# Adding the attention row on GpSimd, evicting it on VectorE, and new due times for the first tiles

## The chip, the cores and the metric

The kernel runs on one core of one Trainium2 chip. The metric is the device time of one execution in microseconds (us), median of several runs; lower is better. The engines are named PE (TensorE), DVE or V (VectorE), ACT (ScalarE), POOL or G (GpSimd) and SP (SyncE, which here issues DMAs). PSUM is the memory that PE writes its products to, SBUF the working memory of all engines.

## What is computed

64 sequences of 128 tokens with 256 features pass one layer of two steps:

```python
# attention step: q, k, v are 16 features wide; correlation over time, 12 best shifts, softmax weights w
q = LN(x) @ Wq + bq;  k = v = ctx @ Wq + bq
corr = mean over batch and feature of ifft(fft(q) * conj(fft(k)))
R = sum over the 12 best shifts of w * roll(v, -shift)      # the same for all 16 heads
x = x + (R repeated 16 times) @ Wout + bout
# feed-forward step; fp4(.) rounds blocks of 16 numbers to a 4-bit grid with one scale per block
xq = fp4(LN(x));  h = silu(xq @ fp4(w_gate).T) * (xq @ fp4(w_up).T)     # 704 wide
x = x + fp4(h) @ fp4(w_down).T
```

Because of the reshape in `R` (batch, heads, 16, time) to (batch, time, 256), the attention step adds to each token a row that depends on few indices only: in this kernel's layout it is one of four matrices `O[0]` to `O[3]`, each 128 x 256 with one more column that holds its mean.

## The kernel before

**Three stages.** In the first (0 to about 55 us) the inputs `xt` and `cx` are read, q, k and the correlation are built on PE, and the weights of the feed-forward step are quantised and transposed. In the second (about 55 to 72 us) the correlation is turned into shifts and weights (`E`, `wm`, `inv`), the weights meet the output matrix (`Wp`), the values are copied from PSUM by ACT (`Va`, L1504), and PE forms the four matrices `O[g]` (L1581). `O[0]` is evicted from PSUM by V, as product times `inv` plus the bias row `Bo` (L1594). For `O[1]` to `O[3]` the bias is brought in by one more product on PE, with one row as its inner size (L1572), and ACT evicts with the scale `inv` (L1588). Before its `Va` copies of g = 1 to 3, ACT loads its table for square roots (L1553); later it loads the table for Silu (L1625).

**The third stage** handles 64 tiles of 128 rows (tile t is row block t % 4 of `X[t // 4]`, and uses `O[(t // 4) % 4]`).

- x part of a group of tiles (`x_parts`): `neg` is minus the new mean (L461); `cc` is x + O + neg. For tiles 0 and 1 (`fast`) V makes `cc` from x and O in one instruction (L472), and x + O itself is added apart. For all others O is first added to `X` (by V at L447 for tiles 2 to 11, two tiles an instruction; by an accumulating DMA issued on GpSimd's queue at L483 from tile 12 on), and ACT makes `cc` (L499). ACT squares and sums (L509), V takes block maxima (`am` L519), reciprocals (`rz` L558), scales `cc` (L586), ACT or V rounds (`k`), V multiplies by the block scales (`xhl` L615). The result is transposed, by PE for tiles 0 to 3 (L631, copied from PSUM at L637 by V for tiles 0 and 1 and by ACT for 2 and 3), by DMA on SP's queue for the rest (L644).
- per tile (`group_ops`): 18 products `gu` on PE (L1224) into one of two PSUM buffers; ACT's Silu gives `g` (L1230); V forms `h` (L1237), which frees the PSUM buffer; V's block maxima `hs` (L1247) read 88 pad columns of `h` that hold a least value, written once per buffer of `h` by three ACT instructions (L1605, key "least"); V's reciprocal `hr` (L1261); GpSimd scales `h` (L1276; V does so for tile 0 and the last ones); ACT rounds (`hk`, `hc`), V multiplies by the scales (`hl` L1329), SP's DMA transposes it into one of eight buffers `hT`, 17 products `pd` on PE (L1373, L1375) follow, V adds to `X` (L1392), SP stores.

**What sets the order.** Nothing runs in the order in which it is written. `S.op(engine, cost, ...)` records each operation with a cost in ns, its reads and writes and a due time `dl`; due times are carried back along the dependences; `plan` then walks through a planned clock and gives each engine, of what is ready within 400 ns, the operation that is due first (operations due inside a window of `RUSH` can hold a place free). `after` is an order without a wait, `chain` forces an operation to follow another on the same engine, `rel` is an earliest time, `late` adds to the planned ready time. Each engine then runs its list in order, and semaphores do the waiting. Where PE's plan has a gap, filler products with `ident` (L726) are written into it.

The due times of the third stage come from one line, with `T0` = 58000, `SLOT` = 5425 and `t` the tile: `at(t) = T0 + SLOT * t`, 4000 earlier for tiles 0 and 1. `gu` of tile t is due at `at(t)`; `pd` is due 4.5 slots later, growing by 6 slots up to tile 56. The x parts are due at 58000 (tiles 0, 1), 65200 (2, 3), 73000 (4 to 7, in one piece), and then by `at`.

Of the kernel before, what the change touches and what calls it, by code (L numbers as in the profile page):

```python
# [23 lines left out]
P = 128  # L24
# [20 lines left out]
WAIT = 400.0  # L45
RUSH = ((10000.0, 40000.0), (41000.0, 73000.0))
SPARE = 400.0
# [213 lines left out]
def xattn_ffn(ctx: ExitStack, tc: tile.TileContext, x, xt, cx, wo, bo, wgu, wd, out):  # L261
# [78 lines left out]
    SLOT = 5425.0  # L340
    LC = 4.5
    GROW = 6.0
# [17 lines left out]
    LA = 4000.0  # L360
    BEFORE = 16
    HOT2 = 70000.0
    ZV, CV, EV = (0, *range(62, 64)), range(61, 64), range(64)
    HPE = (63,)
    GROUPS = [(0,), (1,), *((t, t + 1) for t in range(2, 62, 2)), (62,), (63,)]
    DUE1 = 15000.0
    Q1 = ((0, 4, 0.0, False),)
    TD = 54000.0
# [56 lines left out]

    def x_parts(R, q, i0, nt, fast, due, alu, pe_x=False, root=False, both=None, off=0):
        g, hq = q % 4, q // 4
# [12 lines left out]

        eng = "V"
        pe = fast

        def add(lo, hi):
            def f():
                v = Xq.t[:, i0 + lo : i0 + hi]
                (V if eng == "V" else G).tensor_tensor(v, v, O[g][:, 0:D].unsqueeze(1).broadcast_to([P, hi - lo, D]), ALU.add)  # L447
# [19 lines left out]
        for i in tiles:  # L467
            if fast:
                op(
                    "V",  # L470
                    336,
                    lambda i=i: V.scalar_tensor_tensor(  # L472
                        T["cc"].t[:, i], Xq.t[:, i0 + i], T["neg"].t[:, i : i + 1], O[g][:, 0:D], ALU.add, ALU.add
                    ),
                    r=[(Xq, i0 + i), T["neg"], ("O", g)],
                    w=[(T["cc"], i)],
                )
        if alu == "D":
            for i in tiles:
                adds[4 * q + i] = op(  # L480
                    "G",
                    900,
                    lambda i=i: G.dma_start(Xq.t[:, i0 + i], O[g][:, 0:D], accum_op=ALU.add),  # L483
                    r=[("O", g)],
                    w=[(Xq, i0 + i)],
                    lat=LA,
                    port=False,
                )
                adds[4 * q + i].rel = 0.0
        else:  # L490
            step = 1 if nt == 1 else 2
            for lo in range(0, nt, step):
                add(lo, lo + step)
        for i in tiles:
            if not fast:
                op(
# [664 lines left out]

    T0 = TG

# [34 lines left out]
    def group_ops(tiles):  # L1198
# [10 lines left out]
        def twice(k):  # L1209
            return sub(k).unsqueeze(3).broadcast_to([P, nt, NB, 2])  # L1210

        def at(t):
            return T0 + SLOT * t - (EARLY * (t - END) if t > END else 0.0) - (4000.0 if t < 2 else 0.0)

        for i, t in enumerate(tiles):
# [123 lines left out]
        for i, t in enumerate(tiles):  # L1339
# [30 lines left out]
            def f_d(i=i, hT=hT):  # L1370
# [27 lines left out]
        )  # L1398
        op("SP", 370, lambda: SP.dma_start(out[:, q, i0 : i0 + nt], v()), r=xk, dl=at(tiles[-1]) + SLOT * (LC + GROW * min(t, END) / 64.0 + 2), lat=LL)

# [151 lines left out]
    t1_op = op("A", 450, lambda: A.activation(Wp[:, 1], spec["J", 1][1](), AF.Copy, scale=wv[:, 1:2]), r=[(pv3, "j"), ("wv", 1)], w=[("Wp", 1)])  # L1552
    op("A", 1300, lambda: A.activation(warm, c_half, AF.Sqrt), w=["tbl"], dl=TO, after=[*quick, t1_op])  # L1553
    for e in range(2):
# [8 lines left out]
    d_parts(loaded, (w_op,))  # L1563
    load_x(1, dl=TD + 9000, after=loaded)
    for g in range(4):
        po, pn = ((pdc, "o"), lambda: pdc.t[:, 0 : D + 1]) if g == 0 else ((pa, "o", g), lambda g=g: pa.t[:, 512 * (3 - g) :][:, 0 : D + 1])
        Vg = Va[:, g].rearrange("p (b r e) -> p e (b r)", b=16, e=2)
        if g:
            op(
                "PE",  # L1570
                690,
                lambda pn=pn: PE.matmul(pn(), es[0:1, 0:1].broadcast_to([1, P]), Bo[0:1], start=True, stop=False),  # L1572
                r=["Bo", "es"],
                w=[po],
                after=quick_o,
            )
        first = [
            op(
                "PE",
                560,  # L1580
                lambda e=e, pn=pn, Vg=Vg, g=g: PE.matmul(pn(), Vg[:, e], Wp[:, e], start=(g == e == 0), stop=(e == 1)),  # L1581
                r=[("Va", g), ("Wp", e)],
                w=[po],
            )
            for e in range(2)
        ]
        if g:
            op("A", 450, lambda g=g, pn=pn: A.activation(O[g], pn(), AF.Copy, scale=inv), r=[po, "inv"], w=[("O", g)], dl=TG if g < 2 else TG + SLOT)  # L1588
        else:
            quick_o = first  # L1590
            op(
                "V",
                450,
                lambda pn=pn: V.scalar_tensor_tensor(O[0], pn(), inv, Bo, ALU.mult, ALU.add),  # L1594
                r=[po, "inv", "Bo"],
                w=[("O", 0)],
                dl=TG,
            )

    heat(lambda: hot.t[:, 384:512], (hot, "h"), TG + 7000.0, hot, after=first)  # L1600
    for t in h_tiles:
        op(
            "A",
            350,
            lambda t=t: A.activation(  # L1605
                t[:, :, NF : NF + 2 * NB], ones[:, 0 : 2 * NB].unsqueeze(1).broadcast_to([P, 2, 2 * NB]), AF.Copy, scale=htiny
            ),
            r=[("O", 3)],
            w=["least"],
        )  # L1610
    S.rel = 0.0
    for i, n, e in FIRST:
        x_stage(R4, 0, i, n, True, TG + i * STEP0, e, True, True)
    x_stage(R4, 0, 2, 2, False, TG + 2 * STEP0, "V", True, True)

# [97 lines left out]
```

## Time and profile before

| what | value |
|---|---|
| median of 3 runs | 438.35 us (436.62 to 438.74) |
| the profiled execution: its own time | 436.5 us |
| its span of instructions | 434.6 us |
| busy: PE, DVE, ACT, POOL | 96%, 90%, 66%, 32% |
| first and last product of the feed-forward step | 72.02 us, 431.12 us |
| last `gu` ends | 407.74 us |

The span is what lies between the first and the last instruction; the profiled execution's own time is 1.9 us more. PE's share of busy time includes fillers and products that run at half clock, so it is no measure of useful work: that is 64 times (18 `gu` + 17 `pd`).

### The profile page before, as it was taken

How to read it: one execution, taken by the hardware profiler on the slowest of the kernel's cores; microseconds unless marked ns; L12 is line 12 of the kernel's file. 1: busy time of each engine (PE TensorE's matmuls, PEld its weight loads, DVE VectorE, ACT ScalarE, POOL GpSimd, SP SyncE). 2: the span in 40 equal slices, each digit the busy share in tenths (PEclk: the TensorE clock that was granted, in tenths of full speed). 3: DMA queues.
4: the chain of work that ended last, by engine and by line, in shares of the span. 5: the costliest groups of instructions: out<-in, count | busy, mean ns of one | idle time of the engine just before them, and what ended most of it. 6: DMA issues, size and time to landing. Idle time of an engine off the chain costs nothing.

```text
span 434.6 us, 7990 instructions
## 1 busy us (share of the span) xinstructions
PE 418.9 (96%) x2946; PEld 268.9 (62%) x2946; DVE 392.9 (90%) x855; ACT 285.6 (66%) x480; POOL 137.3 (32%) x122
## 2 busy tenths in 40 slices
PE   8999989899889999999999999999999999999996
PEld 8557666446555656666566666666665666566685
DVE  7999597999999999899999989999999999978862
ACT  3897557978595787467856794887579576364410
POOL 1000002154344354444444444454444222314100
PEclk9999996999999999999999999999999999999999
DMA  8999999453887688489758987697669716942462
GB/s 309 416 419 419 306 224 321 61 111 79 169 151 147 162 179 190 112 134 241 148 121 165 210 141 172 144 160 157 128 151 173 147 40 133 189 116 66 103 162 74
DMA packets 152247, 76.62 MB, mean 176 GB/s; under 512 B 134160, under 2 KB 141712, under 8 KB 152208
## 3 DMA queue, kind: packets, MB, share of 16 engines
q1 hardware_dynamic: 144720, 69.29, 62.5%
q0 software_dynamic: 7488, 6.82, 11.0%
q8 instruction: 23, 0.38, 0.4%
q14 instruction: 16, 0.13, 0.1%
HBM read 27.76 MB, written 8.39 MB: 83 GB/s over the span
## 4 chain that ended last, share of the span: by engine, by line
PE 66%; DVE 16%; ACT 8%; DMA 6%; issue 2%; SPq 1%; ACTq 0%
PE gu L1224 37%; PE pd L1373 14%; PE pd L1375 8%; DMA xt<-in_xt_dram 4%; DVE hs L1247 3%; DVE h L1237 2%; DMA ct<-in_cx_dram 2%; DVE hl L1329 2%; ACT junk L509 1%; ACT g L1230 1%; ACT cc L499 1%; DVE am L519 1%; DVE cc L586 1%; PE gu L1581 1%; ACT hk L1304 1%
## 5 line engine op out<-in xcount | busy, mean ns | idle before, releaser
L1224 PE MATMUL gu<-WgH,xT 128*128 128x512 f16 (+1 forms) x768 | 191.7, 361 | 5.1 <-ACT g L1230 1.9
L1224 PEld LDWEIGHTS <-xT 128*128 128x128 f16 x1152 | 112.4, 98 | 114.5 <-issue 5.1
L1276 POOL TENSOR_TENSOR h<-h,hr 128x704 f32<-128x704 f32 x61 | 92.6, 1519 | 196.3 <-DVE hr L1261 169.3
L1224 PE MATMUL gu<-WgL,xT 128*128 128x512 f16 (+1 forms) x384 | 107.4, 361 | 0.0
L1230 ACT ACTIVATE g<-gu,ug 128x704 f32<-128x704 f32 x64 | 53.7, 840 | 42.0 <-PE gu L1224 41.9
L1304 ACT ACTIVATE hk<-h,c_half 128x1408 int16<-128x1408 f32 (+1 forms) x34 | 47.4, 1395 | 37.3 <-POOL h L1276 34.4
L1247 DVE TENSOR_REDUCE hs<-h 128x44 f32<-128x792 f32 x64 | 66.6, 1041 | 2.1
L1237 DVE SCALAR_TENSOR_TENSOR h<-gu,uh,g 128x704 f32<-128x704 f32 x64 | 55.9, 874 | 5.1 <-ACT g L1230 3.2
L483 POOL DMA_DIRECT2D X<-O x36 | 31.7, 970 | 71.7 <-ACT junk L509 71.7
L1320 ACT ACTIVATE hc<-hk,c_sub 128x1408 f16<-128x1408 int16 (+1 forms) x32 | 45.6, 1426 | 0.5
L1373 PE MATMUL pd<-WdH,hT 128*128 128x256 f16 x352 | 43.7, 273 | 1.2 <-DMA hT<-hl 1.2
L1373 PEld LDWEIGHTS <-hT 128*128 128x128 f16 x352 | 34.3, 98 | 9.5 <-DMA hT<-hl 1.6
L1329 DVE TENSOR_TENSOR hl<-hc,hsb 128x1408 f16<-128x1408 f16 (+1 forms) x34 | 28.6, 842 | 0.2
L1329 DVE TENSOR_TENSOR hl<-hc,hsl 128x1408 f16<-128x1408 f16 (+1 forms) x34 | 28.6, 841 | 0.0
L1261 DVE RECIPROCAL hr<-hs 128x44 f32<-128x44 f32 x64 | 26.8, 418 | 0.2
L509 ACT ACTIVATE junk<-cc 128x256 bf16<-128x256 f32 x64 | 26.0, 406 | 0.4 <-DVE cc L472 0.2
L1375 PE MATMUL pd<-WdL,hT 128*128 128x256 f16 x192 | 26.2, 273 | 0.0
L1290 ACT ACTIVATE hsb<-hs 128x176 bf16<-128x176 f32 (+1 forms) x34 | 11.4, 334 | 19.8 <-DVE hs L1247 19.8
L499 ACT ACTIVATE cc<-X,neg 128x256 f32<-128x256 f32 x46 | 22.5, 499 | 2.9 <-DVE neg L461 2.9
L932 ACT ACTIVATE xsq<-xt,shift 128x1024 f32<-128x1024 f32 x16 | 17.7, 1142 | 8.9 <-DVE shift L928 6.3
L586 DVE TENSOR_TENSOR cc<-cc,rz 128x256 f32<-128x256 f32 x64 | 23.3, 418 | 0.1
L1373 PE MATMUL pd<-WdH,Wdn 128*128 128x256 f16 x176 | 21.8, 273 | 0.7 <-DMA Wdn<-hl 0.7
(254 smaller groups left out, 569.4 us busy)
## 6 DMA issues: line engine op xcount, KB each, us to landing
xt<-in_xt_dram SPq DMA_DIRECT2D x16, 512.0 KB, 8.2
ct<-in_cx_dram SPq DMA_DIRECT2D x7, 1024.0 KB, 12.8
X<-in_x_dram SPq DMA_DIRECT2D x12, 512.0 KB, 4.4
out_dram<-X SPq DMA_DIRECT2D x23, 256.0 KB, 2.3
X<-O POOLq DMA_DIRECT2D x36, 128.0 KB, 3.4
XA<-in_x_dram SPq DMA_DIRECT2D x4, 512.0 KB, 5.3
XA<-O POOLq DMA_DIRECT2D x16, 128.0 KB, 2.7
out_dram<-XA SPq DMA_DIRECT2D x7, 256.0 KB, 2.0
```

Source lines behind the costliest of these rows:

```text
L483: lambda i=i: G.dma_start(Xq.t[:, i0 + i], O[g][:, 0:D], accum_op=ALU.add),
L509: lambda i=i: A.activation(T["junk"].t, T["cc"].t[:, i], AF.Square, accum_out=T["ssq"].t[:, off + i : off + i + 1]),
L1224: PE.matmul(pg.t[:, c0:c1], src[:, b], w[:, k, c0:c1], start=(m == 0), stop=(m == 5))
L1230: lambda pg=pg, g=g: A.activation(g.t, pg.t[:, 0:NF], AF.Silu, scale=ug),
L1237: lambda pg=pg, g=g, i=i: V.scalar_tensor_tensor(B["h"].t[:, i, 0:NF], pg.t[:, NF:NG], uh, g.t, ALU.mult, ALU.mult),
L1247: lambda i=i: V.tensor_reduce(B["s"].t[:, i], B["h"].t[:, i].rearrange("p (jj b e) -> p b jj e", b=NB, e=2), AX.XY, ALU.max, apply_absolut ...
L1276: lambda i=i, zv=zv: (V if zv else G).tensor_tensor(per_block(B["h"].t[:, i, 0:NF], NB), per_block(B["h"].t[:, i, 0:NF], NB), spread(B["r" ...
L1304: lambda: A.activation(sub("k"), sub("h")[:, :, 0:NF], AF.Identity, bias=c_half, scale=24.0),
L1320: lambda: A.activation(flat("c"), flat("k"), AF.Identity, bias=c_sub, scale=SUB),
L1329: lambda e=e, part=part: V.tensor_tensor(B["hl"].t[:, 0:nt, e].rearrange("p t (jj n) -> p t jj n", jj=JJ), sub("c").rearrange("p t (jj n) ...
L1373: PE.matmul(pd, hT.t[:, b], WdH[:, :, b], start=(b == 0), stop=False)
L1375: PE.matmul(pd, hT.t[:, b], WdL[:, :, b], start=False, stop=(b == 5))
```

## The change

1. **O.** The one-row bias products are gone. All four `O[g]` are formed by two products each, in the order g = 0 to 3, and evicted by V as product times `inv` plus `Bo`, due at 58000, 61000, 70000, 70000.
2. **ACT's tables.** The load for square roots no longer follows the `Va` copy of g = 0 and is due 12 us earlier; the load for Silu is due 8 us later.
3. **Adds of O.** For tiles 0 to 11 GpSimd adds O to `X`, one tile an instruction, in the order 2 to 7, 0, 1, 8 to 11 (`GORD`), then come the DMA adds of tiles 12 to 16. The three writes of the least value move from ACT to GpSimd, between the adds of tiles 7 and 0.
4. **Tiles 4 to 7** run as two x parts of two tiles, instead of one of four.
5. **Due times.** `at(t)` starts at 71000 with 3700 a tile up to tile 6, then 5425: 17 us later for tile 0, 2.65 us later from tile 6 on. `pd` is due at `down_at(t)`, 8.6 us later than before for tiles up to 56. `late` of `pd` is zero for tiles 0 to 7, and the forced chain of reciprocal, `h` and `hs` starts at tile 6. The second window of `RUSH` reaches to 90000.

The switches `C1`, `C2E`, `F2` and `cce` of the diff are off in this kernel, and `A0`, `A1`, `A2`, `Q2A` = "P" make `eng` "G" for the adds.

```diff
-RUSH = ((10000.0, 40000.0), (41000.0, 73000.0))
+RUSH = ((10000.0, 40000.0), (41000.0, 90000.0))
...
-    LC = 4.5
+    T0 = 71000.0
+    PACE = 3700.0
+    RAMP = 6
+    FILL = 20000.0
+    LX = 1000.0
+    SL0 = 8
...
+    OD = 3000.0
+    DQ = 2
+    GORD = (2,3,4,5,6,7,0,1,8,9,10,11)
+    LEAST = 5
+    CHAIN = 6
...
+    SILU = 8000.0
+    GA = 800.0
...
-    Q1 = ((0, 4, 0.0, False),)
+    Q1 = ((0,2,0.0,False),(2,2,0.0,False))
...
-        eng = "V"
+        eng = "G" if alu == "P" else "V"
...
-            op(
+            adds[4 * q + i0 + lo] = op(
                 eng,
-                (60 + 270 * n) if eng == "V" else 650 * n if n == 1 else 613 * n,
+                (60 + 270 * n) if eng == "V" else GA * n,
...
-            step = 1 if nt == 1 else 2
+            step = 1 if nt == 1 or eng == "G" else 2
...
+    def at(t):
+        return T0 + PACE * min(t, RAMP) + SLOT * max(t - RAMP, 0) - (EARLY * (t - END) if t > END else 0.0)
+
+    def down_at(t):
+        return T0 + FILL + SLOT * t + SLOT * GROW * min(t, END) / 64.0 - (EARLY * (t - END) if t > END else 0.0)
...
-            if t - 1 in recips:
+            if t - 1 in recips and t >= CHAIN:
...
-                late=SLACK if t < END else 0.0,
-                dl=at(t) + SLOT * (LC + GROW * min(t, END) / 64.0 + nt - 1 - i + (LATE if t >= END else 0)),
+                late=SLACK if SL0 <= t < END else 0.0,
+                dl=down_at(t) + SLOT * (nt - 1 - i + (LATE if t >= END else 0)),
...
-    op("A", 1300, lambda: A.activation(warm, c_half, AF.Sqrt), w=["tbl"], dl=TO, after=[*quick, t1_op])
+    op("A", 1300, lambda: A.activation(warm, c_half, AF.Sqrt), w=["tbl"], dl=TO - 12000.0, after=[t1_op])
...
-        if g:
-            op(
-                "PE",
-                690,
-                lambda pn=pn: PE.matmul(pn(), es[0:1, 0:1].broadcast_to([1, P]), Bo[0:1], start=True, stop=False),
...
-        if g:
-            op("A", 450, lambda g=g, pn=pn: A.activation(O[g], pn(), AF.Copy, scale=inv), r=[po, "inv"], w=[("O", g)], dl=TG if g < 2 else TG + SLOT)
...
+        op(
+            "V",
+            450,
+            lambda g=g, pn=pn: V.scalar_tensor_tensor(O[g], pn(), inv, Bo, ALU.mult, ALU.add),
+            r=[po, "inv", "Bo"],
+            w=[("O", g)],
+            dl=(TG, TG + OD, TG + 12000.0, TG + 12000.0)[g],
+        )
...
+    least = [
+        op(
+            "G",
+            500,
+            lambda t=t: G.tensor_scalar(
+                t[:, :, NF : NF + 2 * NB], ones[:, 0 : 2 * NB].unsqueeze(1).broadcast_to([P, 2, 2 * NB]), htiny, None, ALU.mult
             ),
...
-    x_stage(R4, 0, 2, 2, False, TG + 2 * STEP0, "V", True, True)
+    x_stage(R4, 0, 2, 2, F2, at(2) - LX, A2, P2, True, cce=C2E)
...
-        x_stage(R4, 1, i, n, False, TG + DUE1 + d, "V", p, True)
-    op("A", 1300, lambda: A.activation(warm, c_half, AF.Silu), w=["tbl"], dl=TG)
+        x_stage(R4, 1, i, n, False, at(4 + i) - LX, A1, p, True, cce=C1)
+    op("A", 1300, lambda: A.activation(warm, c_half, AF.Silu), w=["tbl"], dl=TG + SILU)
...
+    row = [adds[t] for t in (*GORD, *range(12, 17)) if t in adds and adds[t].eng == "G"]
+    for o, u in zip(row, row[1:]):
+        u.after.add(o)
+    for o in least:
+        o.after.add(row[LEAST])
+        row[LEAST + 1].after.add(o)
```

More of the change, by code (lines that the diff above doesn't have):

```diff
@@ L361, in xattn_ffn @@
     BEFORE = 16
+    OD = 3000.0
[3 more added lines that the diff above has]
+    CHAIN = 6
+    Q2A = "P"
+    A0 = "P"
+    A1 = "P"
+    A2 = "P"
+    C1 = None
+    C2E = None
+    F2 = False
+    P2 = True
+    DUE2 = 7200.0
+    SILU = 8000.0
+    GC = 1060.0
+    GA = 800.0
     HOT2 = 70000.0
@@ L424, in roots, with x_parts @@
         op("V", 75, lambda: V.scalar_tensor_tensor(t, v, TINY / 4.0 / -3.2, y, ALU.mult, ALU.mult), r=[bv, by], w=[bt])
-    def x_parts(R, q, i0, nt, fast, due, alu, pe_x=False, root=False, both=None, off=0):
+    def x_parts(R, q, i0, nt, fast, due, alu, pe_x=False, root=False, both=None, off=0, cce=None):
         g, hq = q % 4, q // 4
@@ L467, in x_parts @@
         for i in tiles:
-            if fast:
+            if fast or cce == "V":
                 op(
@@ L479, in x_parts @@
             for i in tiles:
-                adds[4 * q + i] = op(
+                adds[4 * q + i0 + i] = op(
                     "G",
@@ L488, in x_parts @@
                 )
-                adds[4 * q + i].rel = 0.0
+                adds[4 * q + i0 + i].rel = 0.0
         else:
-            step = 1 if nt == 1 else 2
+            step = 1 if nt == 1 or eng == "G" else 2
             for lo in range(0, nt, step):
@@ L494, in x_parts @@
         for i in tiles:
-            if not fast:
+            if cce == "G":
+                op(
+                    "G",
+                    GC,
+                    lambda i=i: G.tensor_scalar(
+                        T["cc"].t[:, i], Xq.t[:, i0 + i], T["neg"].t[:, i : i + 1], None, ALU.add
+                    ),
+                    r=[(Xq, i0 + i), T["neg"]],
+                    w=[(T["cc"], i)],
+                )
+            elif not fast and cce != "V":
                 op(
@@ L1160, in xattn_ffn @@
     pp2 = ctx.enter_context(tc.tile_pool(name="pp2", bufs=1, space=PSUM))
-    T0 = TG
+    def at(t):
+        return T0 + PACE * min(t, RAMP) + SLOT * max(t - RAMP, 0) - (EARLY * (t - END) if t > END else 0.0)
+    def down_at(t):
+        return T0 + FILL + SLOT * t + SLOT * GROW * min(t, END) / 64.0 - (EARLY * (t - END) if t > END else 0.0)
     WgHf = WgH.rearrange("p h c n -> p h (c n)")
@@ L1210, in twice @@
             return sub(k).unsqueeze(3).broadcast_to([P, nt, NB, 2])
-        def at(t):
-            return T0 + SLOT * t - (EARLY * (t - END) if t > END else 0.0) - (4000.0 if t < 2 else 0.0)
         for i, t in enumerate(tiles):
@@ L1398, in group_ops @@
         )
-        op("SP", 370, lambda: SP.dma_start(out[:, q, i0 : i0 + nt], v()), r=xk, dl=at(tiles[-1]) + SLOT * (LC + GROW * min(t, END) / 64.0 + 2), lat=LL)
+        op("SP", 370, lambda: SP.dma_start(out[:, q, i0 : i0 + nt], v()), r=xk, dl=down_at(tiles[-1]) + 2 * SLOT, lat=LL)
     Vn = cs.tile([P, 4, 16, 16], F32, name="Vn")
@@ L1564, in xattn_ffn @@
     load_x(1, dl=TD + 9000, after=loaded)
+    quick_o = ()
     for g in range(4):
@@ L1567, in xattn_ffn @@
         Vg = Va[:, g].rearrange("p (b r e) -> p e (b r)", b=16, e=2)
-        if g:
-            op(
-                "PE",
-                690,
[L1572 to L1576, printed above, removed]
         first = [
@@ L1580, in xattn_ffn @@
                 560,
-                lambda e=e, pn=pn, Vg=Vg, g=g: PE.matmul(pn(), Vg[:, e], Wp[:, e], start=(g == e == 0), stop=(e == 1)),
+                lambda e=e, pn=pn, Vg=Vg, g=g: PE.matmul(pn(), Vg[:, e], Wp[:, e], start=(e == 0), stop=(e == 1)),
                 r=[("Va", g), ("Wp", e)],
                 w=[po],
+                after=quick_o,
             )
@@ L1586, in xattn_ffn @@
         ]
-        if g:
[L1588 to L1598, printed above, removed]
+        quick_o = first
+        op(
[5 more added lines that the diff above has]
+            dl=(TG, TG + OD, TG + 12000.0, TG + 12000.0)[g],
+        )
     heat(lambda: hot.t[:, 384:512], (hot, "h"), TG + 7000.0, hot, after=first)
-    for t in h_tiles:
+    least = [
         op(
[L1603 to L1606, printed above, removed]
+            "G",
+            500,
+            lambda t=t: G.tensor_scalar(
+                t[:, :, NF : NF + 2 * NB], ones[:, 0 : 2 * NB].unsqueeze(1).broadcast_to([P, 2, 2 * NB]), htiny, None, ALU.mult
             ),
-            r=[("O", 3)],
             w=["least"],
-        )
+            after=first,
+            dl=TG + 12000.0,
+        )
+        for t in h_tiles
+    ]
     S.rel = 0.0
     for i, n, e in FIRST:
-        x_stage(R4, 0, i, n, True, TG + i * STEP0, e, True, True)
-    x_stage(R4, 0, 2, 2, False, TG + 2 * STEP0, "V", True, True)
+        x_stage(R4, 0, i, n, True, TG + i * STEP0, A0, True, True)
+    x_stage(R4, 0, 2, 2, F2, at(2) - LX, A2, P2, True, cce=C2E)
     X_homes += [xs.tile([P, 4, D], F32, name=f"X{n}") for n in range(2, 6)]
@@ L1629, in xattn_ffn @@
             load_x(q)
-            due = T0 + SLOT * (4 * q - min(MARGIN, LEAD[0] + LEAD[1] * q))
-            parts.append((due, x_parts(R4, q, 0, 4, False, due, "D" if q > 2 else "V", both=both, off=4 * n)))
+            due = at(4 * q) - SLOT * min(MARGIN, LEAD[0] + LEAD[1] * q)
+            parts.append((due, x_parts(R4, q, 0, 4, False, due, "D" if q > DQ else Q2A, both=both, off=4 * n)))
         for n, (due, part) in enumerate(parts):
```

## Prediction, made before the changed kernel ran

> **What bounds the kernel now.** I read the page first, then stretches of time, then the chain that ended last around the change, then the order of time of the engines there.
>
> The stretches (busy time of PE, PEld, DVE, ACT, POOL, then the granted clock) say where PE is not full:
>
> ```profile
> 60.00:65.00 5.00, 3.61 (x13) 2.14 (x14) 4.86 (x14) 3.95 (x12) 0.00 (x0) 1.00 1.17 246
> 65.00:70.00 5.00, 4.86 (x13) 3.33 (x12) 3.57 (x14) 2.66 (x9) 0.00 (x0) 0.54 1.09 212
> 70.00:75.00 5.00, 4.91 (x27) 2.98 (x26) 3.39 (x11) 4.67 (x16) 1.50 (x3) 0.77 1.02 406
> 75.00:80.00 5.00, 4.93 (x30) 2.39 (x28) 4.93 (x16) 4.94 (x10) 3.05 (x4) 1.00 1.08 211
> 80.00:85.00 5.00, 4.27 (x28) 2.44 (x26) 4.96 (x10) 4.33 (x9) 0.00 (x0) 1.00 0.01 3
> 85.00:90.00 5.00, 3.68 (x22) 2.02 (x22) 4.96 (x10) 4.95 (x13) 0.03 (x1) 1.00 0.46 105
> 200.00:300.00 100.00, 99.88 (x634) 61.94 (x633) 95.75 (x188) 75.65 (x136) 45.32 (x39) 1.00 0.84 171
> ```
>
> From 200 us on PE is the bound and V follows with 4 to 8% to spare. From 75 to 140 V is full (63.8 of 65 us, adding its rows) and PE waits. I summed the spaces over 0.12 us between neighbouring `gu` and `pd` products (L1224, L1373, L1375), fillers not counted: 9.45 us in 11 places: 1.60 at 79.4, 2.21 at 85.0, then 1.25, 0.69, 0.75, 0.93, 0.97 between 108 and 173, 0.12 at 273, and 0.93 after 380. So the span of 434.6 is 72.0 until the first `gu`, 349.6 of feed-forward products, 9.45 of spaces, 3.5 after the last. Only the 72.0 and the 9.45 can move. The chain (start, us, what) shows what sets the 72.0:
>
> ```profile
> 60.17 1.28 ACT L1553
> ...
> 61.67 0.82 ACT Va L1504 x3
> ...
> 62.53 0.69 PE gu L1572 x2
> ...
> 66.46 0.49 ACT O L1588
> ...
> 66.99 1.22 PE gu L1572 x2
> 68.21 2.01 PE gu L1581 x4
> 70.22 0.85 PE gu L726 x4
> 71.08 0.44 PE pd L631 x4
> ```
>
> It runs through a table load, bias products, an ACT eviction and fillers, none of which tile 0 needs. Tile 0 is late only because its transposes (L631) stand in PE's queue behind them. In order of time:
>
> ```profile
> 67.53 0.42 DVE L615 TENSOR_TENSOR xhl<-k,slo 128x512 f16<-128x512 f16 x1
> 71.54 0.42 DVE L637 COPY xT<-pd 128x512 f16<-128x512 f16 x1 [2.86 <-PE pd L631]
> 80.50 1.89 DVE L447 TENSOR_TENSOR X<-X,O 128x512 f32<-128x512 f32 x3
> 81.02 0.61 PE L1224 MATMUL gu<-WgH,xT 128*128 128x512 f16 x2 [0.73 <-ACT xT L637]
> 81.34 0.45 ACT L1605 ACTIVATE h<-ones,htiny 128x176 f32<-128x176 f32 x1
> 82.31 1.03 DVE L1247 TENSOR_REDUCE hs<-h 128x44 f32<-128x792 f32 x1
> 87.19 0.59 PE L1224 MATMUL gu<-WgH,xT 128*128 128x512 f16 x2 [1.32 <-DVE h L1237]
> ```
>
> `xhl` is ready at 67.95 and the transposes start at 70.87. `hs` of tile 0 starts 1.7 us after its `h`, once ACT's third least value is written; V adds O meanwhile. PE waits at 87.19 for an `h` that V forms behind work for tiles 4 to 7.
>
> **Part by part.**
>
> *O and the table load.* ACT is idle for 1.23 us before its first `Va` copy (59.78). The load (1.28 + 0.20) now goes there: the first copy comes 0.3 us later, the fourth ends at about 61.3 instead of 62.48. Three bias products go (2.6 us of PE, one of them at half clock). `O[0]` ends at about 61.65; three more times four passes of 0.217 spacing end at 64.3, where the last now ends at 70.22. The transposes then meet a free PE (fillers excepted) when `xhl` is ready.
>
> *V's path for tiles 0, 1.* 0.3 later from `Va`, about 0.3 earlier since the add at 63.83 (0.68) no longer stands before L552; three evictions on V (0.487 each from L1594, 1.5 us) fit where V idles: 0.6 us while ACT takes the roots, 2.86 at 68.7. So `xhl` stays near 67.95, the first `gu` comes 1.15 later as now: 69.1. GpSimd's adds could hold V's step back; no row shows that, between 0 and 0.8 us. The clock could stay half until the first `gu`s are over: 0 to 1.5 us (3 us of them at half rate). I take 0.5 together: start 69.6, **-2.4 us** (ends -3.2 and -0.9).
>
> The clock fell from 65.4 to 72.3 after a stretch with PE 3.61 of 5 us busy, part of it one-row products. [...]
>
> *GpSimd's adds.* Gone from V: six L447 of 0.684, 4.1 us, three of them before `hs` of tile 0. One add of 128x256 on GpSimd: the nearest row is its own scaling of 128x704 at 1.52 us (L1276); by elements 0.55, at most 1.52; I take 0.65, since the row is the same kind of operation. Twelve and three least values (about 0.5, as on ACT) are 9.3 us from 62.3 on, so the list ends near 72, with room for waits on `O`. GpSimd idled until 73.5; behind the list stand the DMA adds of tiles 12 to 16 (first at 73.5 now) and its first scaling, at 90. If the cover is gone and an add costs 1.52, the list ends near 82 and costs PE nothing directly. ACT's `cc` of tiles 2 and 3 starts near 64.6 instead of 66.83, where it stands behind the eviction of `O`; that of 4 to 7 near 66 instead of 71.33.
>
> *ACT* loses three evictions (0.474) and three least values (0.437), 2.7 us, and gains 1.3 by the split (two roots of 0.29, a second pair of roundings 2 x 0.28, a cast). The Silu load must follow the roots of tiles 4 to 7 as before; those come about 3 us earlier, so `g` of tile 0 moves from 78.3 to about 74.
>
> *The split of tiles 4 to 7* costs V 1.6 us: half-size rows against whole ones, such as `am` 2 x 0.69 for 1.21, `xhl` 4 x 0.42 for 2 x 0.68, `rz` 2 x 0.35 for 0.55. It costs SP's queue one more transpose, which lands 3.8 us after issue and is due after V's part.
>
> *Due times.* V's work for 4 to 7 was due at 73.0 and stood before `h` of tile 1; now 84.8 and 92.2, against 82.1 for the `gu` that needs that `h`. Between 61.4 and 87.15 V worked 22.5 us before that `h` was out; without six adds (4.1) and half of tiles 4 to 7 (4), with evictions and some of the split (2), it is 16.4. With 3 us of waits `h` of tile 1 is out near 81, where PE, 69.6 plus three times 3.6, asks for it at 80.4. The spaces of 1.60 and 2.21 shrink to about 1.5 together: **-2.3** (ends -3.8 and 0).
>
> *The later spaces* (4.7 us to 273): V is full there, and PE now asks 2.4 us earlier. V's balance is 3.04 us that it idled between 65 and 75, plus 4.1 - 1.5 - 1.6 = 1.0; less what GpSimd holds back. That just pays for the 4.7 us won above, at nothing held back. I take **+0.6** (ends -2 and +3).
>
> *The tail.* From tile 6, `pd` is due 8.6 us later and `gu` 2.65: one slot more between them, so one more `pd` (1.86 us) is kept for the end, where PE now has 0.93 of spaces: **-0.4** (ends -0.8 and +1.0).
>
> Sum: -2.4 - 2.3 + 0.6 - 0.4 = -4.5; ends -9.8 and +3.1. On the execution's own 436.5: 432.0. The median of before lies 1.85 above that execution, so 433.8.
>
> **Rivals.** A change of 0.5% (2.2 us) is about what a measurement of this kernel can tell from none: below 436.2 is faster, above 440.5 slower.
>
> *Given back on V.* PE starts earlier, but V, full to 140, serves tile k no sooner. Gain: 3.0 + 1.0 less half of GpSimd's 9.3 us as V's waits, 4.6: -0.6 to +0.6, about 438. For it: 63.8 of 65. Against: the two large spaces come from order, not from V's total. A start that fails to move ends here too.
>
> *Slower: V and GpSimd exclude each other.* All 61 of GpSimd's scalings lie beside `h` and `hs` on V, none beside a V step with two SBUF operands (L586, L615, L1329); the order does that, so the trace can't price a clash. The adds run from 62 to 72 among just such steps of tiles 0 to 3, in no chain. If V stands still for half of GpSimd's time and an add costs 1.0 to 1.52, V loses 6.8 to 9.9 against its 4.0: +2.8 to +5.9, about 442.5. It decides from 4 us of V's waiting on. Against: V idles 3 us in those ten.
>
> [...]
>
> **How the numbers follow.** Forecast 0.70, its own range 429.5 to 437; given back 0.18 (436.5 to 440); slower 0.12. From 429.5 to 440.0 what is left out is most of the slower rival and a small part of the forecast with large gains. Faster: 0.67 of the forecast and 0.04 of the second case. Same: 0.03 + 0.14 + 0.01. Slower: 0.11.
>
> **What the changed profile would show.** Right: transposes (L631) following `xhl` at once, first `gu` near 69.6; no one-row products; `hs` of tile 0 right after its `h`; GpSimd's adds of about 0.65 from 62 on; spaces before 90 of at most 2 us. Wrong: clock half during the first `gu`s; V's two-input steps starting only at the end of GpSimd's adds; new spaces before tile 4; the spaces from 100 to 173 grown by more than 3 us.

## The result: 440.46 us, 0.95% slower

The changed kernel took 440.46 us (median of 12 runs, 439.6 to 445.5), the kernel before 437.4 in as many runs beside it (434.88 to 438.74). The ratio is 1.0095, 95% interval 1.0066 to 1.0124: slower. The forecast was 433.8 with a range up to 440.0, and "slower" had 0.11; it was added to a before of 438.35, and on 437.4 it would be 432.9.

Top of the page of the changed kernel: the span, the busy time of the engines, and the group of GpSimd's adds (busy in all, mean ns of one).

```profile
span 438.3 us, 8039 instructions
PE 419.1 (96%) x2958; PEld 268.2 (61%) x2958; DVE 396.0 (90%) x862; ACT 284.8 (65%) x479; POOL 149.8 (34%) x137
...
L469 POOL TENSOR_TENSOR X<-X,O 128x256 f32<-128x256 f32 x12 | 9.0, 778 | 64.8 <-DVE O L1619 64.8
```

Six adds left V and three bias products left PE, and the engines' shares are within two points of what they were; they tell nothing here. The span does, cut as in the prediction (spaces: over 0.12 us between neighbouring `gu` and `pd` products):

| us | before | after | forecast step | measured |
|---|---|---|---|---|
| first `gu` starts | 72.02 | 73.14 | -2.4 | +1.1 |
| spaces to 135 us | 7.42 | 5.30 | -2.3, and part of +0.6 | -2.1 |
| later spaces | 2.03 | 3.36 | the rest of +0.6, part of -0.4 | +1.3 |
| feed-forward products | 349.66 | 353.11 | 0 | +3.45 |
| after the last product | 3.49 | 3.39 | | -0.1 |
| span | 434.6 | 438.3 | -4.5 | +3.7 |

The stretches of the changed kernel (busy PE, PEld, DVE, ACT, POOL, then the granted clock):

```profile
65.00:70.00 5.00, 2.71 (x20) 2.48 (x20) 4.89 (x14) 3.87 (x15) 4.29 (x6) 1.00 1.01 203
70.00:75.00 5.00, 2.65 (x14) 1.25 (x15) 4.92 (x15) 3.23 (x15) 2.75 (x4) 0.86 0.98 380
75.00:80.00 5.00, 5.00 (x22) 2.17 (x21) 4.75 (x15) 4.08 (x9) 4.72 (x8) 0.80 0.38 131
...
100.00:110.00 10.00, 7.71 (x38) 4.07 (x37) 10.00 (x16) 5.25 (x6) 6.30 (x6) 0.83 0.81 114
```

V, which idled 3 us between 65 and 75 before, is full there now, and yet PE stands still for 4.6 of those 10 us, and again for 2.3 of the ten from 100: V's work takes longer. PE's two pauses (from 68.4 to 71.3, with two shorter ones up to 73.1, and from 101.1 to 103.8) are each followed by half clock, which is what stretches the products (0.80 and 0.83 in the rows; the half-rate spans are 73.6 to 77.0 and 104.3 to 107.7). The order of time on VectorE shows what became longer; each row joins neighbouring instructions of one line (the xN at its end):

```profile
62.02 0.49 DVE L1619 SCALAR_TENSOR_TENSOR O<-pd,inv,Bo 128x257 f32<-128x257 f32 x1
62.81 1.70 DVE L494 SCALAR_TENSOR_TENSOR cc<-X,neg,O 128x256 f32<-128x256 f32 x2
65.54 1.60 DVE L483 TENSOR_SCALAR neg<-MT,O 128x2 f32<-128x2 f32 x3
67.66 1.32 DVE L618 TENSOR_TENSOR cc<-cc,rz 128x256 f32<-128x256 f32 x2
71.20 0.95 DVE L647 TENSOR_TENSOR xhl<-k,slo 128x512 f16<-128x512 f16 x1
```

The kernel before, the second and the fourth of these:

```profile
62.18 0.88 DVE L472 SCALAR_TENSOR_TENSOR cc<-X,neg,O 128x256 f32<-128x256 f32 x2
65.04 0.76 DVE L586 TENSOR_TENSOR cc<-cc,rz 128x256 f32<-128x256 f32 x2
```

One by one, the two `cc` take 0.83 and 0.94 us (0.49 and 0.48 before), `neg` of 128x2 up to 0.79 (0.22), the second `cc` by `rz` 0.95 (0.42), `xhl` 0.95 (0.42). What GpSimd does in the same microseconds:

```profile
62.59 1.64 POOL L469 TENSOR_TENSOR X<-X,O 128x256 f32<-128x256 f32 x2 [60.79 <-DVE O L1619]
65.70 2.99 POOL L469 TENSOR_TENSOR X<-X,O 128x256 f32<-128x256 f32 x4 [1.47 <-DVE O L1619]
68.69 2.50 POOL L1630 TENSOR_SCALAR h<-ones,htiny 128x176 f32<-128x176 f32 x3
71.16 1.59 POOL L469 TENSOR_TENSOR X<-X,O 128x256 f32<-128x256 f32 x2
```

The steps that grew by 0.35 us or more all lie beside an add; the steps that ran beside the least values alone grew by at most 0.22. Between 61 and 80 us, the steps that take over 0.1 us more than the shortest of their kind in the two kernels exceed it by 4.4 us in all; before it was 0.1. So `xhl` of tile 0 is ready at 72.16 instead of 67.95: `O[0]`'s eviction starts 0.6 us later, and from there to `xhl` V takes 10.14 us instead of 6.56. PE follows at once, on an input that comes 4.2 us late:

```profile
71.34 0.29 PE L663 MATMUL pd<-ident_h,xhl 128*128 128x128 f16 x2 [2.94 <-DVE xhl L647]
...
73.14 0.64 PE L1259 MATMUL gu<-WgH,xT 128*128 128x512 f16 x2 [0.42 <-DVE xT L669]
...
103.83 0.59 PE L1259 MATMUL gu<-WgH,xT 128*128 128x512 f16 x2 [2.29 <-DVE h L1272]
```

The transposes do follow `xhl` directly, as forecast, and the 2.92 us that they waited in PE's queue before are gone; but with `xhl` 4.2 us later the start lost 1.1 us instead of winning 2.4.

### The profile page after: what moved, and what is told of

Same layout as the page of the kernel before. It is cut to its first block, busy times and chain, and to the rows that moved or that the text cites. A ratio compares the mean times of both kernels' runs of the same rounds, so it can differ in the third digit from the quotient of the medians.

```text
span 438.3 us, 8039 instructions
## 1 busy us (share of the span) xinstructions
PE 419.1 (96%) x2958; PEld 268.2 (61%) x2958; DVE 396.0 (90%) x862; ACT 284.8 (65%) x479; POOL 149.8 (34%) x137
## 4 chain that ended last, share of the span: by engine, by line
PE 62%; DVE 18%; ACT 8%; DMA 8%; issue 3%; SPq 1%; POOL 0%; DVEq 0%; POOLq 0%; ACTq 0%
PE gu L1259 37%; PE pd L1408 13%; PE pd L1410 7%; DMA xt<-in_xt_dram 4%; DVE hs L1282 3%; DVE h L1272 3%; DMA ct<-in_cx_dram 2%; DVE hl L1364 2%; DVE cc L618 2%; DVE xhl L647 1%; ACT g L1265 1%; DMA xT<-xhl 1%; ACT hk L1339 1%; ACT junk L541 1%; DVE hr L1296 1%
## 5 line engine op out<-in xcount | busy, mean ns | idle before, releaser
L1259 PE MATMUL gu<-WgH,xT 128*128 128x512 f16 (+1 forms) x768 | 193.8, 364 | 6.4 <-DVE h L1272 2.3
L1259 PE MATMUL gu<-WgL,xT 128*128 128x512 f16 (+1 forms) x384 | 109.1, 366 | 0.0
L469 POOL TENSOR_TENSOR X<-X,O 128x256 f32<-128x256 f32 x12 | 9.0, 778 | 64.8 <-DVE O L1619 64.8
L632 ACT ACTIVATE k<-cc,c_half 128x1024 int16<-128x1024 f32 (+1 forms) x17 | 18.2, 1069 | 11.0 <-DVE cc L618 10.9
```

The lines of the kernel that those rows point to most:

```text
L1259: PE.matmul(pg.t[:, c0:c1], src[:, b], w[:, k, c0:c1], start=(m == 0), stop=(m == 5))
```

## The experiments

Two theories. **Blocking**: GpSimd's new work and V's steps hold each other up; without the blocking the forecast holds. **Order**: the new due times and the split load V or reorder it so that it serves PE later, whatever GpSimd does. A third, **clock**: the loss is the half-rate spans. V's balance is given as the length from `O[0]`'s eviction to the start of the eighth `h`, and in it the busy time, the stretch (what the steps take over the shortest duration of their kind, added up) and the idle time.

### Blocking alone

**Adds cut to 4 of 256 columns** (on the changed kernel; every engine's order stays the same, and most of O's add for tiles 0 to 11 is left out):

```diff
-(V if eng == "V" else G).tensor_tensor(v, v, O[g][:, 0:D].unsqueeze(1).broadcast_to([P, hi - lo, D]), ALU.add)
+G.tensor_tensor(v[:, :, 0:4], v[:, :, 0:4], O[g][:, 0:4].unsqueeze(1).broadcast_to([P, hi - lo, 4]), ALU.add)
```

> The changed kernel with GpSimd's twelve adds of O cut to 4 of their 256 columns; the order of all engines is unchanged, so x is left without most of O for tiles 0 to 11 in what follows. Theory A (VectorE and GpSimd block each other): VectorE's steps between 62 and 72 us lose their stretch of about 3 us (cc back to 0.48 from 0.83 and 0.94, neg to 0.22 from 0.78), the first gu comes near 70.5 instead of 73.1, PE's pause before the transposes shrinks below 1.5 us and the clock may stay full; the time falls by 3 to 5 us against the changed kernel, to the level of before or 1 us under it. Theory B (VectorE's new order: evictions and neg steps ahead of tile 0): VectorE's rows lose their stretch but the first gu stays above 72.5 and the time falls by less than 1 us.

Measured: 435.99 us, ratio 0.999 (0.9962 to 1.0019), 4.6 us below the changed kernel by the two ratios. First `gu` 69.73 (forecast of the step: 69.6), no half clock after it (granted 1.00 from 70 to 90). VectorE of this run in order of time, the same instructions as above:

```profile
62.53 0.88 DVE L494 SCALAR_TENSOR_TENSOR cc<-X,neg,O 128x256 f32<-128x256 f32 x2
64.44 0.54 DVE L483 TENSOR_SCALAR neg<-MT,O 128x2 f32<-128x2 f32 x3
65.49 0.78 DVE L618 TENSOR_TENSOR cc<-cc,rz 128x256 f32<-128x256 f32 x2
68.33 0.41 DVE L647 TENSOR_TENSOR xhl<-k,slo 128x512 f16<-128x512 f16 x1
```

1.70 became 0.88, 1.60 became 0.54, 1.32 became 0.78, 0.95 became 0.41. Nothing but the duration of GpSimd's adds differs, so the loss of the start comes from them: from `O[0]`'s eviction to `xhl` V takes 7.00 us here, 3.1 less than in the changed kernel and 0.4 more than before. The 4.6 us of time are no price of the blocking alone, since most of the adds' work is left out.

**The chain of reciprocal, `h`, `hs` from tile 0 on again** (on the changed kernel):

```diff
-    CHAIN = 6
+    CHAIN = 0
```

> The changed kernel with the forced chain of reciprocal, h and hs from the first tile on (CHAIN = 0 instead of 6). Theory A: GpSimd's scalings of tiles 1 to 5 lie beside h and hs again, so that VectorE's int16 steps of 1.10 and 1.83 us at 100 and 108 us go back to 0.4 and 0.5; the pause of 2.74 us at 101 us and the half clock after it go; 1.5 to 3.5 us faster than the changed kernel, first gu unchanged at 73. Theory B: no change over 1 us, since VectorE is full there either way.

Measured: 439.11 us, ratio 1.0049 (1.0024 to 1.0074). First `gu` 72.79: the start stays late. What it mends is the part from 95 to 110, where GpSimd's scalings of tiles 1 to 5 met V's `L338`. VectorE of the changed kernel:

```profile
100.22 1.10 DVE L338 TENSOR_SCALAR k<-k 128x1024 int16<-128x1024 int16 x1
...
108.45 1.83 DVE L338 TENSOR_SCALAR hc<-hc 128x1408 int16<-128x1408 int16 x1
```

and with the chain:

```profile
101.80 0.41 DVE L338 TENSOR_SCALAR k<-k 128x1024 int16<-128x1024 int16 x1
...
105.72 0.52 DVE L338 TENSOR_SCALAR hc<-hc 128x1408 int16<-128x1408 int16 x1
```

The scaling at 108.39 beside the second of them takes 1.51 us; V's step waits it out nearly whole. With the chain 60 of GpSimd's 61 scalings lie beside an `h` again, as before; in the changed kernel 57 do. The interval overlaps that of the changed kernel, so the 1.35 us between the medians is no firm size; the stretch is.

**Both together** (the two edits above, on the changed kernel; the same part of the adds is left out):

> The changed kernel with the chain from the first tile on and GpSimd's twelve adds cut to 4 of 256 columns (x lacks most of O for tiles 0 to 11 in what follows); the order is that of the run with the chain alone (439.1). If the two blocks add up: 439.1 less 4 to 4.5, so 434.5 to 435, with VectorE's stretch up to its eighth h at the level of before. If VectorE has other limits there: 435.5 to 437, no better than the small adds alone (436.0).

Measured: 435.56 us, ratio 0.996 (0.9931 to 0.9989). V's balance adds up:

| | length | busy | of it stretch | idle |
|---|---|---|---|---|
| before | 52.1 | 48.5 | 2.9 | 3.6 |
| after | 54.4 | 53.2 | 9.7 | 1.2 |
| adds cut | 49.9 | 49.3 | 5.8 | 0.6 |
| chain | 52.3 | 51.1 | 6.7 | 1.2 |
| both | 48.5 | 47.3 | 3.1 | 1.2 |

Of the 6.8 us of new stretch the adds make 3.9 (9.7 less 5.8), the missing chain 3.0 (9.7 less 6.7), and with both gone it is at the old level. (With the shortest durations in the two kernels as the measure the three are 6.6, 3.9 and 2.7.) This is what the blocking theory says of V, and the order theory has no place for it. But by the ratio the time is 1.75 us below before, though most of O's add is left out, and not the 4.5 of the forecast: blocking isn't all that was missed. The median lies at the edge of the expectation's second case, and the interval overlaps that of the adds cut alone, so the chain's share shows in V's balance and not firmly in the time.

**GpSimd's adds in the kernel before** (nothing else of the change):

```diff
-    FIRST = ((0, 2, "V"),)
+    FIRST = ((0, 2, "P"),)
...
-            step = 1 if nt == 1 else 2
+            step = 1 if nt == 1 or eng == "G" else 2
...
-    x_stage(R4, 0, 2, 2, False, TG + 2 * STEP0, "V", True, True)
+    x_stage(R4, 0, 2, 2, False, TG + 2 * STEP0, "P", True, True)
...
-        x_stage(R4, 1, i, n, False, TG + DUE1 + d, "V", p, True)
+        x_stage(R4, 1, i, n, False, TG + DUE1 + d, "P", p, True)
```

("P" is an add on GpSimd, one tile an instruction; tiles 8 to 11 have it too.)

> The kernel before with one edit: the adds of O for tiles 0 to 11 on GpSimd, one tile an instruction; products with the bias, ScalarE's evictions and all due times as before. Theory A (block): VectorE's steps beside the adds stretch by 0.3 to 0.6 us each, 2 to 4 us in all from 62 to 85 us, more or less the 4.1 us that leave VectorE: between 1 us faster and 3 us slower than before. Theory B (adds are free, order is all): 2 to 4 us faster.

Measured: 438.55 us, ratio 1.003 (1.0013 to 1.0047). Its VectorE and GpSimd at the start:

```profile
62.43 1.70 DVE L472 SCALAR_TENSOR_TENSOR cc<-X,neg,O 128x256 f32<-128x256 f32 x2
```

```profile
62.21 3.18 POOL L447 TENSOR_TENSOR X<-X,O 128x256 f32<-128x256 f32 x4 [60.42 <-DVE O L1594]
```

The same 1.70 in the other kernel. V is rid of 4.1 us of adds and the kernel is still 0.3% slower, with the first `gu` at 73.67 though `xhl` is ready at 68.84: the transposes still stand behind the bias products and the fillers there.

**The changed kernel with its adds on V**, the least values before the first DMA add, without and with the chain:

```diff
-    Q2A = "P"
-    A0 = "P"
-    A1 = "P"
-    A2 = "P"
+    Q2A = "V"
+    A0 = "V"
+    A1 = "V"
+    A2 = "V"
...
-        o.after.add(row[LEAST])
-        row[LEAST + 1].after.add(o)
+        row[0].after.add(o)
```

The second of the two has `CHAIN = 0` besides.

> The changed kernel with the adds of O for tiles 0 to 11 on VectorE again (two tiles an instruction), the least values at the head of GpSimd's list. Theory A: the first gu near 70.5, no half clock at the first gu products, 2 to 4 us faster than the changed kernel although VectorE carries 4.1 us more. Theory B: VectorE has still the evictions and neg steps ahead and 4.1 us more work: equal or up to 3 us slower than the changed kernel.

> The changed kernel with the adds on VectorE and the forced chain from the first tile on. What stays of the change is O, the tables, the split of tiles 4 to 7, the least values on GpSimd and the due times. If the missing chain (GpSimd's scalings beside VectorE's int16 steps) made the spaces of 15.5 us in the kernel with adds on VectorE: spaces near 12 and 2 to 3 us faster than that kernel's 440.9, so 438. If the due times and the split made them: no more than 1 us faster.

Measured: 440.94 us, 1.0096 (1.0062 to 1.0131), and 439.66, 1.0051 (1.0029 to 1.0073). The first `gu` is at 69.40 and 69.66, and yet nothing is won: the spaces are 15.5 and 12.1 us instead of 9.45. Here the order theory has its evidence: in the second, V's stretch is at the level of before, and the kernel is slower all the same. The runs under "The parts by themselves" put that on the split in the new order more than on the due times.

Side by side, the two places of the adds cost the same: 1.0095 on GpSimd and 1.0096 on V without the chain, 1.0049 and 1.0051 with it. V gives up 4.1 us of adds and loses 3.9 us beside them; moving them brought neither gain nor loss in time. What the blocking took is the gain that the forecast counted on; what makes the kernel slower than before is the rest, the missing chain and the split.

### The clock

**Ten filler products before the transposes of tile 0** (on the changed kernel), to keep PE busy in its pause:

```diff
+    for _ in range(10 if fast and i == 0 else 0):
+        PE.matmul(hot.t[:, 384:512], ident, ident, start=True, stop=True)
```

> The changed kernel with ten more filler products (2.1 us at full clock) on PE ahead of the transposes of tile 0, in the pause of 2.94 us that ends at 71.34; nothing else moves. If the half clock after 73.6 us comes of that pause, it goes, the first gu stays at 73.1, and the first gu products take 1.7 us less: 1.0 to 1.7 us faster where VectorE can follow, 0 to 0.5 where VectorE is full. If the clock falls for another reason, the half clock stays and the time does not move.

Measured: 443.32 us (439.3 to 444.2), ratio 1.0116 (1.0078 to 1.0155). Its profiled execution had no half clock at all in the third stage; its stretches:

```profile
70.00:75.00 5.00, 3.29 (x24) 1.93 (x24) 4.92 (x17) 3.23 (x15) 2.99 (x4) 1.00 1.00 386
...
100.00:110.00 10.00, 7.71 (x50) 4.76 (x48) 10.00 (x17) 6.96 (x14) 6.30 (x6) 1.00 0.80 129
```

The products took 350.17 us, 2.9 less than in the changed kernel, and the spaces 11.54, 2.9 more; the span is 438.5 against 438.3. At full clock PE waits as long as it ran slow: V, 10.00 of 10 us, decides. In this pair of executions, then, the half clock follows from the pauses and is not itself the loss. Why most of the other runs of this kernel took 443 to 444, at a mean granted clock of 0.988, I can't say.

### The parts by themselves

**O and the table load alone** (on the kernel before: no bias products, V evicts all four, the early load; adds, split and due times as before):

```diff
-        if g:
-            op("A", 450, lambda g=g, pn=pn: A.activation(O[g], pn(), AF.Copy, scale=inv), r=[po, "inv"], w=[("O", g)], dl=TG if g < 2 else TG + SLOT)
...
+            lambda g=g, pn=pn: V.scalar_tensor_tensor(O[g], pn(), inv, Bo, ALU.mult, ALU.add),
+            r=[po, "inv", "Bo"],
+            w=[("O", g)],
+            dl=(TG, TG + 3000.0, TG + 12000.0, TG + 12000.0)[g],
```

> The kernel before with the change to O alone: no one-row products, all four O evicted by VectorE with the bias, the table load for square roots ahead of the Va copies; adds of O stay on VectorE, least values on ScalarE, due times as before. My step for the start: the first gu near 69.5 to 70 instead of 72.0 and 1.5 to 3 us faster than before. If it was wrong by itself (the evictions delay VectorE's path to tile 0): first gu at 71.5 or later and no gain.

Measured: 435.65 us, ratio 0.9975 (0.9956 to 0.9994). PE in order of time:

```profile
69.47 0.60 PE L1224 MATMUL gu<-WgH,xT 128*128 128x512 f16 x2 [0.48 <-DVE xT L637]
...
80.06 0.61 PE L1224 MATMUL gu<-WgH,xT 128*128 128x512 f16 x2 [1.48 <-ACT xT L637]
```

The first `gu` is 2.55 us earlier and the spaces to 135 us are 9.01 instead of 7.42; the pause of 3.29 before tile 2 is new, and half clock follows it (the pair of products at 80.51 took 0.91 us; at full clock a pair takes 0.59). Of the start's gain 1.6 us are given back in spaces, and V serves the later tiles no sooner: its eighth `h` starts at 114.05, before at 113.52. By the ratio the gain is 1.1 us, under the 1.5 to 3 expected. (The trace is of the slowest of 13 executions, 437.5 us; the last kernel below has the same pause of 3.29 and no half clock after it, at a mean granted clock of 1.000.)

**The split of tiles 4 to 7 alone, and the least values on GpSimd alone** (each on the kernel with O alone; the second orders them before the DMA adds):

```diff
-    Q1 = ((0, 4, 0.0, False),)
+    Q1 = ((0, 2, 0.0, False), (2, 2, 0.0, False))
```

```diff
-            "A",
-            350,
-            lambda t=t: A.activation(
+            "G",
+            500,
+            lambda t=t: G.tensor_scalar(
...
+    for o in least:
+        row[0].after.add(o)
```

> The change to O and the tables alone (435.65) plus one more part: tiles 4 to 7 as two x parts of two tiles, due as before. VectorE carries 1.6 us more there. If VectorE's balance decides: 1 to 2 us slower than 435.65. If the split lets tile 4 start sooner and that counts: equal or up to 1 us faster.

> The change to O and the tables plus the three least values on GpSimd, at the head of its list; all else as before. They cost GpSimd 2.5 us beside VectorE's steps for tile 0. If that block counts: first gu 0.5 to 1 us later than 69.5 and up to 1 us slower than 435.65; but hs of tile 0 no longer waits for ScalarE. If only the second counts: 0.5 to 1.5 us faster.

**Adds of tiles 0, 1 and 8 to 11 by DMA** (on the kernel with O alone; least values on ACT, ordered behind the `Va` copies), and the same with x parts ordered earlier by `LEAD`:

```diff
-    FIRST = ((0, 2, "V"),)
+    FIRST = ((0, 2, "D"),)
...
-            parts.append((due, x_parts(R4, q, 0, 4, False, due, "D" if q > 2 else "V", both=both, off=4 * n)))
+            parts.append((due, x_parts(R4, q, 0, 4, False, due, "D", both=both, off=4 * n)))
```

```diff
-    LEAD = (0.5, 0.5)
+    LEAD = (2.5, 0.5)
```

> A version of the kernel before with the change to O and the tables, the adds of tiles 0, 1 and 8 to 11 by accumulating DMA from GpSimd's queue (as for later tiles) instead of VectorE or GpSimd, the adds of tiles 2 to 7 on VectorE, and the least values written by ScalarE between its Va copies and the first squares, where it idles 1.7 us; chain, split and due times as before. By theory A no step of VectorE is held back and 2 us of adds leave it before hs of tile 0: first gu near 69.5, spaces of 9 or less, 1 to 3 us faster than the change to O alone (435.65), so 433 to 434.5.

> The version with DMA adds for tiles 0, 1 and 8 to 11 and early least values, with the x parts of tiles 8 to 11 due 10.8 us earlier (LEAD 2.5 instead of 0.5), since the pause of 8.06 us in the version without it was a wait for the transpose of tile 8, whose steps VectorE ran 5 us later than before. If that was all: the pause goes, spaces of 6 to 8 us, 432 to 434. If the DMA adds themselves come too late: a pause stays ahead of tile 8 and the time stays over 437.

Measured: split 441.53, 1.0119 (1.0088 to 1.0151); least values 440.5, 1.008 (1.0054 to 1.0106); DMA adds 441.39, 1.0094 (1.007 to 1.0117). None of the three says anything of its part, for the same reason. PE's longest waits (us in all, times, longest) in the split, the DMA adds, and the DMA adds with `LEAD`:

```profile
PE gu L1224 <- DMA xT<-xhl: 7.8, 2, 7.5
```

```profile
PE gu L1224 <- DMA xT<-xhl: 8.3, 2, 8.1
```

```profile
PE gu L1224 <- DMA xT<-xhl: 2.7, 2, 2.3
```

In each of the three (7.0 us with the least values on GpSimd) the planner let V's x part of tiles 8 to 11 slip behind one more `h`, and PE waited 7 to 8 us for tile 8's transpose. With `LEAD` the DMA adds take 437.55, 1.0007 (0.9989 to 1.0026): the long pause is gone, but so is the expected 432 to 434, with spaces of 10.05 us. So the old order priced a slip, not the part; the split is priced inside the new order below.

**Due times and O, without GpSimd's adds, split and least values** (on the changed kernel: adds on V, chain, one x part for tiles 4 to 7, least values on ACT):

```diff
-    CHAIN = 6
+    CHAIN = 0
...
-    Q1 = ((0,2,0.0,False),(2,2,0.0,False))
+    Q1 = ((0,4,0.0,False),)
```

(with the adds as in the kernels with adds on V above.)

> The change to O and the tables plus the new due times (at, down_at, the later Silu load, no late for the first pd, the longer RUSH window); adds on VectorE, least values on ScalarE, tiles 4 to 7 in one piece, chain from the first tile. If the due times are what is left of the loss in the kernel with adds on VectorE and the chain (439.7): 438 to 440. If split and least values on GpSimd made it: 435 to 436.

Measured: 437.2 us, ratio 0.9996 (0.9976 to 1.0016), above O alone by 1.5 us by the medians and 0.9 by the ratios, whose intervals overlap: the due times by themselves won nothing, and no loss by them is firm. The spaces before 95 us are 1.82, 1.71 and 2.74, against 3.81 in the two of before: moved, not gone.

**DMA adds for tiles 0, 1 and 8 to 11 and V's for the rest in the changed kernel**, with chain and with the least values on ACT, split and whole (the last two lines are the whole one's alone):

```diff
-    Q2A = "P"
-    A0 = "P"
-    A1 = "P"
-    A2 = "P"
+    Q2A = "D"
+    A0 = "D"
+    A1 = "V"
+    A2 = "V"
...
-    Q1 = ((0,2,0.0,False),(2,2,0.0,False))
+    Q1 = ((0,4,0.0,False),)
```

> The changed kernel with all of its work and neither block: adds of tiles 0, 1 and 8 to 11 by accumulating DMA, of tiles 2 to 7 on VectorE, least values on ScalarE before the first squares, chain from the first tile; split and due times as changed. VectorE has 1.4 us of adds more than in the small-adds kernels: 435.5 to 437.5. If the due times and the split cost by themselves: 438 or more.

> As the one before, with tiles 4 to 7 in one x part. The split costs VectorE 1.6 us by its rows: if VectorE's balance decides, 0.5 to 1.5 us faster than the kernel with the split; if the earlier start of tile 4 is worth more, slower by as much.

Measured: 439.63, 1.0057 (1.0033 to 1.0081), and whole 436.19, 0.9977 (0.9955 to 0.9998). The split costs 3.4 us; V's busy time to the eighth `h` is only 0.5 longer (49.8 against 49.3), its idle time 1.6 (3.6 against 2.0). No other pair here shows the split by itself; the kernel with adds on V and the chain (439.66) differs from the one before these two (437.2) by the split and by the least values on GpSimd, and is 2.4 us slower by the ratios. Both speak for the order theory.

**O alone, with the adds of tiles 0 and 1 by DMA** (on the kernel with O alone):

```diff
-    FIRST = ((0, 2, "V"),)
+    FIRST = ((0, 2, "D"),)
```

> The change to O and the tables alone (435.65), with one more edit: the adds of tiles 0 and 1 by accumulating DMA, one VectorE step of 0.68 us less ahead of hs of tile 0; the rest of VectorE's order stays. 0.3 to 0.8 us faster than 435.65, so about 435.1, if VectorE's balance decides there; no change if not.

Measured: 435.84 us, ratio 0.9973 (0.9953 to 0.9994). This one, O alone and the one with DMA adds and tiles 4 to 7 whole are the three that compute everything and lie below both kernels, by about 0.25% of before: they are not told apart from each other, and a difference of that size is under the 0.5% set in the prediction.

## Why the prediction was wrong

**The step that failed** is "GpSimd's adds could hold V's step back ... between 0 and 0.8 us". The adds held V back 3.9 us, 3.1 of it on tile 0's own path, and the chain's absence, which stands in the change but was never priced, 2.7 to 3.0 more. So the 4.1 us of adds that left V were paid for in full, and the kernel with them on V is as fast (1.0096 against 1.0095). A second term was too small: the split, 1.6 us in V's balance, cost 3.4 us of time. I had seen that all 61 scalings lay beside `h` and `hs`, and that nothing could price a clash; I took the empty stretch of V (3 us idle) as cover, though the adds were ordered exactly among the steps on tile 0's path. Idle time of V elsewhere covers nothing there.

**The rival "V and GpSimd exclude each other"**, given 0.12, is what happened. It put V's loss at 6.8 to 9.9 us; the new stretch is 6.8. It put the profiled execution 2.8 to 5.9 above before; it is 3.6 above (440.08 against 436.5). That the numbers meet is in part luck: it let V lose half the time of adds of 1.0 to 1.52 us each; V lost 3.9 of the 9.0 us of adds of 0.778, and the other 3.0 beside scalings, which it doesn't name; and part of the 3.6 us is the split's. The rows show the wait for some steps only: beside an add `cc` took 0.83 and 0.94 us for 0.49 and 0.48, and a V step beside a scaling waited nearly to its end (`L338` at 108.45, 1.83 for 0.52). `hs`, beside most of the scalings, took 1.04 us in both kernels; and with the adds cut, the two `cc` by `rz` from 65.49 lie beside the writing of the least values, which reads `ones` and runs from 65.25 to 67.76, and took 0.78 us together (0.76 before), with no such wait.

**O and the table load, start 69.6**: right as a step. 69.47 with O alone, 69.73 with the short adds. In the change itself PE's last product of `O[0]` ended at 61.98 instead of about 61.65, and the eviction ran from 62.02 to 62.51, 0.6 us later than before: V was 0.4 us late already near 55.9 and then waited 0.31 for ACT's `E`, which I had not followed.

**Add of 0.65**: 0.72 to 0.91, mean 0.778. **Least values of 0.5**: 0.72 to 1.03 each, 2.50 us for three; ACT's duration was no guide to GpSimd's. The adds end at 78.1 instead of 72, the last four after a wait of 2.5 us for V's `O`; the DMA adds of tiles 12 to 16 begin there, and PE lost nothing by that directly, as forecast.

**The two large spaces, -2.3**: the number came out for the wrong reason. They are 0.28 and 1.35 in the changed kernel, but because PE asks 1.1 us later and runs at half clock; a new one of 2.74 at 101.1, a wait for `h` of tile 4, takes their place. Without the blocking (both removed) the spaces are 9.54 in all, against 9.45, with one of 2.96 at 88.5: the due times moved them. The argument "order, not V's total" against the rival "given back on V" was the error. O alone shows that rival by itself: 2.55 won at the start, 1.6 given back in spaces. Its price for the adds, half of GpSimd's time as V's waits, was close too (3.9 of 9.0 us).

**V's balance of 1.0**: right if nothing is held back. Busy 47.3 to the eighth `h` with both blocks removed, against 48.5, and the idle time shrank as forecast. It isn't gain enough: the forecast's -4.5 needed the spaces to go.

**The split's 1.6 us on V**: its busy time rose 0.5 in the one pair that shows it, but the time 3.4.

**The tail, -0.4**: not there; spaces after 380 are 0.92 against 0.93.

**Clock half during the first `gu`s**, named as a sign of being wrong, came, for 3.4 us, and again at 104. The profiled execution with fillers is as long without it, so here, where V is full, it cost little by itself.

## What to carry to other kernels

Before moving work to GpSimd, list V's instructions in the microseconds where it will run, above all those on the path to the next stage: here V lost 3.9 us to 9.0 us of adds, as much as it had given up. An ordering rule that looks like tuning of V alone (here the chain that kept scalings beside `h` and `hs`) may be what keeps the engines apart; price its removal as an addition of GpSimd work. And where an engine is full for 60 us, an earlier start of its consumer becomes waits later, so count the gain only up to that engine's idle time, and try a part in the order that it will run in, since a slip of one tile's transpose alone made PE wait 7 to 8 us.

## What the runs showed of the hardware

- A V step on a tiny tile waits too: `neg` of 128x2, 0.22 us alone, took 0.78 and 0.79 beside an add. And an int16 TENSOR_SCALAR with a single tile input waited 1.3 us (1.83 for 0.52).
- Half clock came without a wholly idle stretch. The half-rate spans of the two traces lie on a grid of 3.41 us: in the changed kernel they run from 73.59 to 77.00 and from 104.31 to 107.72, nine lengths from start to start, and before one of two lengths runs from 65.43 to 72.26. The span from 70.18 to 73.59 held 1.24 us of PE work and the next was at half rate, and a pause of 2.74 at 101.1 had the same effect (1.12 us of work in its span of the grid). The length of a pause doesn't decide alone: with the fillers PE is busy for the same 7.71 of the ten us from 100, and the clock stayed at 1.00 there, where the changed kernel had a mean of 0.83; and the pause of 3.29 before tile 2 was followed by half clock with O alone and not in the last kernel, whose profiled execution had a mean granted clock of 1.000. Nor does one amount of work part the two cases: in the changed kernel spans with 1.63 us (from 66.76) and 1.89 (from 63.35) were followed by full clock, and in the kernel before one with 2.90 (from 62.02; 1.4 us of it one-row products) by half clock, one with 2.08 (from 126.87) by full clock.
- The kernel before spreads with its mean granted clock: runs at 1.000 took about 434.9 us, at 0.996 436.3, at 0.991 437.1, at 0.987 438.6 (those at 0.992, 437.9, lie out of this order), so, by an estimate from these times, about 1.2 us for each half-rate span (3.41 us at half rate take 0.004 off the mean over 435). That is a correlation of runs, and as large as half of the differences looked for here.
